# A fixed order from attention into the experts: second expert's weights in the keys' place, four early tiles of it before the last rows

## The chip, the cores and the metric

The kernel runs on one core of a Trainium2 chip. The metric is the device time in microseconds of one execution, as the median of several runs. Beside the plain runs there is one execution under the hardware profiler, from which all durations of instructions come.

## The reference

One transformer block over 4096 tokens (2 sequences of 2048, width 256) in float32. First attention with 16 heads of 64 in a causal window of 128 keys, then a mixture of 8 experts with two chosen for each token, both behind a layer norm whose scale and shift come from a small modulation vector:

```python
h = _layernorm(x) * (1 + ca) + sa
x = x + ga * attention(h, Wqkv, Wout)          # window of 128, softmax
h = _layernorm(x) * (1 + cb) + sb
probs = softmax(h @ gate_w.T + gate_b); topk_prob, topk_idx = top_k(probs, 2)
for c in range(2):                             # first and second choice
    pos  = how many earlier tokens chose the same expert as choice c
    keep = pos < 640                           # capacity
    hmid = relu(rows @ W1[e] + b1[e])          # 256 -> 1024
    y   += (hmid @ W2[e] + b2[e]) * prob * keep
x = x + gb * y
```

A token's place in its expert's buffer depends on all tokens before it. So the router of the last tokens is known only when attention and its output projection for them are done.

## The kernel before

**Numbers.** Each float32 operand is split into a high and a low part in the fp32r format (`split`: ScalarE casts the high part, a second engine subtracts it for the low part), and each product is made of three matmuls (`passes`, L203). The weights are loaded in pieces of 512 KB into two staging buffers (tag `raw`) and split from there.

**Attention.** The 4096 tokens are 16 groups `g` of 256. Work runs in iterations `w` = 0 to 63, each for two of the eight head pairs of a group; an iteration of the steady state takes 10.6 to 11 us. `iteration(w)` writes four ages of work beside one another: projections for w+1, scores of w, exponentials and scaling of w-1, transposes and values of w-2, output projection of w-3. Three more iterations, 64 to 66, empty this pipeline. The projections' weights `wq` lie in the tag `big` of pool `bigw`, the keys `kr` in the attention pool. The last projections of queries and keys are in w=62, those of values in w=63.

**Router.** `close(g)` is a generator of about ten steps for one group: residual (L620, L621), norm, transposes `tp_f`, logits `pl`, first and second choice, running counts `pref` and the matmuls `cnt`, slots, and at last four indirect DMAs on POOL (L785) that scatter the rows into `xbuf` in DRAM, where each expert has its region of 1280 rows. `place` gives each step an iteration and a point in it (letters A, B, H, C), `go` runs what is placed there. The last two groups are treated apart so that some rows can be read before they are known: `shift` moves late rows of expert 0 behind its first four tiles of 128 rows (`EARLY`), whose area the late scatters leave alone.

**Experts.** Work is cut into `items`: some tiles of one expert. Expert 0 has items 0 to 4 of two tiles each, experts 1 to 6 begin with an item of six tiles, and expert 7 with one of four. An item turns its rows (`turn_slots`, matmuls `tp_x`, split into `xT`), multiplies eight slices `f` of the first layer (`ph`; ReLU on ScalarE L904 and VectorE L905; low part L906, which for item 0 is POOL's), and two slices later the second layer (`y`). `results` adds the bias, `scale_of` makes each row's factor `gw` and destination `tok`, and `give` multiplies and adds the rows into the output by indirect DMAs on POOL (L967, L968). Items 0, 1, 2 and the head of each further expert always run; others run if `fill`, the count of rows, says so (`further`, L1178, behind a branch). With these inputs expert 0 and expert 1 have six tiles at most.

**Order.** Iterations 0 to 63 are written in a manual schedule: PE, ACT, DVE and POOL do their work in the order of the program. From iteration 64 on the framework's scheduler sets each engine's order, except where the program raises a priority (`go`) or keeps an order. Expert 0's weights go to the tag `big`, expert 1's to a tag `odd` of the expert pool `mp`, which opens when attention's pools close. The halves of expert 1's first matrix are split by ScalarE and POOL in items 1 and 2. SP issues nearly all loads and the output write of `close`, one behind the other; each waits there for its buffer and for what it reads.

Of the kernel before, what the change touches and what calls it, by code (L numbers as in the profile page):

```python
# [28 lines left out]
def adaln_block_kernel(  # L29
# [38 lines left out]


    EARLY = 4 * P  # L70
    WIDE = 6
# [32 lines left out]
    tokid = const.tile([P, NT], I32, name="tokid")  # L104
    shift = const.tile([P, 1], FP, name="shift")
    fill = const.tile([P, E], I32, name="fill")
# [25 lines left out]

    def load_split(hi, lo, src, shape, name, scale=None, pool=stage, eng=nc.vector, keep=False):
        raw = pool.tile(shape, FP, tag="raw", name=f"raw_{name}", bufs=2)
        nc.sync.dma_start(out=raw, in_=src)
        split(hi, lo, raw, scale, eng, keep)

    def load_expert(e, pool, tag):

        w = pool.tile([P, 2, ND * FF + NF * D], FR, tag=tag, name=f"we_{e}", bufs=1)  # L140
        wa = w[:, :, 0 : ND * FF].rearrange("p a (k f) -> p a k f", k=ND)
        wb = w[:, :, ND * FF :].rearrange("p a (k d) -> p a k d", k=NF)

        def pieces():
            for i in range(2):
                s = slice(i * FF // 2, (i + 1) * FF // 2)
                load_split(
                    wa[:, 0, :, s], wa[:, 1, :, s], w1[e, :, s].rearrange("(k p) f -> p k f", p=P),
                    [P, ND, FF // 2], f"w1_{e}_{i}", keep=e > 0, eng=nc.gpsimd if e == 1 else nc.vector,
                )  # L150
                yield
            for i in range(2):
                s = slice(i * NF // 2, (i + 1) * NF // 2)
                load_split(
                    wb[:, 0, s, :], wb[:, 1, s, :],
                    w2[e, i * FF // 2 : (i + 1) * FF // 2, :].rearrange("(k p) d -> p k d", p=P),
                    [P, NF // 2, D], f"w2_{e}_{i}", keep=e > 0,
                )
                yield

        return wa, wb, pieces()

# [7 lines left out]
    within = aw.tile([P, P], I32, name="within")  # L170
    kr = aw.tile([P, 2, NP, 2 * SBT, P], FR, name="kr")
    cols = aw.tile([P, 2, ND, B], FP, name="cols")
# [433 lines left out]
    def close(g):  # L606
# [60 lines left out]
        def tile2(name, n=SBT):  # L667
            return small.tile([P, n], FP, tag=name, name=f"{name}_{g}", bufs=2)
# [54 lines left out]

        if g == NG - 2:

            total = totals(j0, n)
            nc.vector.tensor_scalar(shift, total[:, 0:1], -1.0, float(EARLY), ALU.mult, ALU.add)
            nc.vector.tensor_scalar(shift, shift, 0.0, None, ALU.max)
        nc.tensor.matmul(out=cnt[:, 0:n], lhsT=tri, rhs=ohf, start=True, stop=False)
# [41 lines left out]
        if late:  # L771
            rows_of = NSLOT - EARLY
            sel = tile2("sel", SBT * KC)
            nc.vector.tensor_scalar(
                sel, pk, float(E * P), shift[:, 0:1], ALU.is_equal, ALU.mult
            )
            nc.vector.tensor_tensor(pos_, pos_, sel, ALU.add)

# [19 lines left out]
        if g == NG - 1:  # L798

            total = totals(NT, n)  # L800
            nc.vector.tensor_tensor(total[:, 0:1], total[:, 0:1], shift, ALU.add)
            nc.vector.tensor_copy(fill, total)
# [4 lines left out]


    items = []
    for e in range(E):  # L810
        head = 2 if e == 0 else 4 if e == E - 1 else WIDE
        ends = [0, *range(head, NB + 1, 2)]
        items += [(e, range(lo, hi)) for lo, hi in zip(ends, ends[1:])]
# [7 lines left out]
    def load_b2(e):  # L821
        pool = mp if e else const
        b2s[e] = pool.tile([P, D], FP, tag="b2", name=f"b2_{e}")
        nc.sync.dma_start(out=b2s[e], in_=b2[e : e + 1, :].to_broadcast([P, D]))
# [19 lines left out]
    def turn_slots(q, n0):  # L844

        tiles = items[q][1]
        if n0 == 0:
            w = len(tiles)
            if q and (w > 2 or items[q - 1][0] == E - 1 and items[q - 1][1].start == 0):
                w = WIDE  # L850
            xTs[q] = [
                (mp if q else early).tile([P, ND, w * P], FR, tag=f"xT{i}{w}", name=f"xT{i}_{q}")
                for i in range(2)
            ]
        m = min(2, len(tiles) - n0)
        if m <= 0:
            return
        tp = bank(f"tp_x{q}_{n0}")
        tpv = tp.rearrange("p (d s) -> p d s", d=ND)
        for n in range(m):  # L860
            for d in range(ND):
                turned = nc.tensor.transpose(
                    tpv[:, d, n * P : (n + 1) * P], xts[q][:, n0 + n, d * P : (d + 1) * P], ident
                )
                if q > 5:
                    tc.keep_in_program_order(turned)
        s = slice(n0 * P, (n0 + m) * P)
        split(xTs[q][0][:, :, s], xTs[q][1][:, :, s], tpv[:, :, 0 : m * P])

    def first_layer(q, f):  # L870
        e, tiles = items[q]
        wa = experts[e][0]
        xh, xl = xTs[q]
# [13 lines left out]
        for i in range(nw):  # L887
# [17 lines left out]
            nc.vector.tensor_scalar(r[:, s], phv, bias, 0.0, ALU.add, ALU.max)  # L905
        (nc.vector if q else nc.gpsimd).tensor_tensor(hl, r[:, 0:W], hh, ALU.subtract)  # L906
        hms[q, f] = (hh, hl)

    def second_layer(q, f, only=None):
        e, tiles = items[q]  # L910
        wb = experts[e][1]
        hh, hl = hms[q, f]
# [50 lines left out]
    def give():  # L963
# [27 lines left out]
    NW = NU // 2  # L991
    VALUES = [(0, 0), (1, 0), (0, 1), (1, 1)]

    NORM = ["0B", "1A", "1H", "2A", "2B"]
    CLOSE = ["0H", "1A", "1B", "2H", "3H", "4A", "4B", "5H", "6A", "6C"]
    LATE = {
        NG - 3: ["0H", "1A", "1B", "2H", "3H", "4A", "4B", "4H", "4C", "4C"],
        NG - 2: ["0H", "1A", "1B", "2H", "2H", "2C", "2C", "3H", "3C", "3C"],
        NG - 1: ["0H"],
# [7 lines left out]
    for g in range(NG):  # L1007
# [3 lines left out]
        place(last, g * (NP // 2) + 6, LATE.get(g, CLOSE))  # L1011

    def go(w, at):
        for work in places.pop((w, at), ()):
            if w < NW:
                next(work, None)
            else:
                with tc.high_priority():
                    next(work, None)

    def first_item():
        turn_slots(0, 0)
        yield
        for f in range(NF + LAG):
            if f < NF:
                first_layer(0, f)
            if f >= LAG:
                second_layer(0, f - LAG)
            yield
        results(0, 0, 2)  # L1030

# [3 lines left out]
    def iteration(w):  # L1035
# [37 lines left out]
        if w < NW:  # L1073
            project_v(g, *VALUES[p2])
        if done[1]:
# [19 lines left out]

    STEPS = {NW: 3, NW + 1: 4, NW + 2: 4}
    start = first_item()
    experts = {}
    part(*project_qk(0, 0, 1))
    everything = {mybir.EngineType.PE, mybir.EngineType.Activation, mybir.EngineType.DVE, mybir.EngineType.Pool}  # L1100
    with tc.manual_schedule(engines=everything):
        for w in range(NW):
            iteration(w)
            if w == NW - 2:
                load_b2(0)
                load_slots(0)
    experts[0] = load_expert(0, bigw, "big")
    for _ in experts[0][2]:
        pass
    for w in range(NW, NW + 3):  # L1110
        iteration(w)
        if w == NW + 2:
            load_slots(1)
        for _ in range(STEPS[w]):
            next(start, None)
    for _ in start:
        with tc.high_priority():
            next(last, None)
    for _ in last:
        pass  # L1120
    give()
# [5 lines left out]
    ring.update(pool=pm_, bufs=2)  # L1127
    experts[1] = load_expert(1, mp, "odd")
    load_b2(1)
    turn_slots(1, 0)  # L1130

    def item(q, steps):
# [26 lines left out]
    def start_expert(e):  # L1159
        if e < E and e not in experts:  # L1160
            experts[e] = load_expert(e, *((bigw, "big") if e % 2 == 0 else (mp, "odd")))
            load_b2(e)

    def piece(e):
        start_expert(e)
        if e < E:
            next(experts[e][2], None)

# [6 lines left out]
    def further(q):  # L1175

        e, tiles = items[q]
        with tc.If(filled[e] > tiles.start * P):  # L1178
# [5 lines left out]
    filled = []  # L1184
    item(
        1,
        {
            **{f: [do(piece, 1)] for f in range(2)},
            2: [do(load_slots, 2, 2)],
            4: [do(load_slots, 5)],  # L1190
            7: [do(turn_slots, 2, 0)],
        },
    )
    item(
        2,
        {
            0: [do(piece, 1)],
            1: [do(piece, 1)],
            7: [do(turn_slots, 3, 0)],
            4: [do(turn_slots, 5, 0)],  # L1200
            5: [do(turn_slots, 5, 2), fills],
            6: [do(turn_slots, 5, 4)],
        },
    )
    further(3)
    heads = [q for q in range(5, NI) if items[q][1].start == 0]
    for q, q2 in zip(heads, heads[1:] + [NI]):
# [38 lines left out]
```

## Time and profile before

| | |
|---|---|
| median of 3 runs | 1177.53 us (1176.76 to 1178.51) |
| the profiled execution's own time | 1175.13 us |
| its span, first to last instruction | 1173.1 us |
| mean granted clock of TensorE | 0.967 |
| busy: PE, DVE, ACT, POOL | 93%, 74%, 58%, 51% |
| scores of w=62 begin | 722.78 us |
| last group's residual ends | 769.97 us |
| first multiplication of item 1 | 790.26 us |
| first multiplication of item 2 | 808.66 us |
| first multiplication of expert 1 (six tiles) | 829.23 us |
| first multiplication of expert 2 | 868.41 us |

The profiled execution and its span differ by 2 us that lie outside the instructions. Times of events count from the first instruction. An engine's share of busy time is a mean over stages that have different limits; "busy" of TensorE contains time at a lowered clock, in which the same matmul takes longer.

### The profile page before, as it was taken

The numbers are of one execution on the slowest core, as the hardware profiler recorded it, in microseconds if no ns is written. First come the engines' busy times: TensorE is split into PE (matmuls) and PEld (weight loads), VectorE is DVE, ScalarE is ACT, GpSimd is POOL, SyncE is SP. The second block draws the span as 40 slices with busy tenths as digits, with TensorE's granted clock in tenths as the row PEclk, the third lists the DMA queues.
The fourth block names the chain that finished last, engine by engine and source line by source line (L and its number), as shares of the span: only waits on it lengthen the run. The fifth ranks groups of instructions, "written<-read, shape, count | busy, mean of one in ns | idle before, by whom it ended". The sixth has DMA issues, their size and how long they took to land. (4 is left out here: it accounts for less than half of the span.)

```text
span 1173.1 us, 25151 instructions
## 1 busy us (share of the span) xinstructions
PE 1090.8 (93%) x9244; PEld 1003.0 (86%) x9244; DVE 864.5 (74%) x2130; ACT 678.8 (58%) x2097; POOL 601.7 (51%) x777
## 2 busy tenths in 40 slices
PE   6899999999999989999999999868899999999995
PEld 4688888888988879889889888658899999999995
DVE  6556778778778777787787787758578777877774
ACT  4467677776776657777777676514344344444441
POOL 4235474674674555665665665554234606343524
PEclk9799999999999989999999999778899999999998
DMA  6991010010010010000000001315234524352413
GB/s 230 226 200 36 7 33 19 24 36 19 21 39 19 21 37 25 29 23 23 26 23 23 27 15 34 91 39 163 73 113 103 86 85 90 79 92 64 82 47 36
DMA packets 59571, 72.09 MB, mean 61 GB/s; under 512 B 4807, under 2 KB 51152, under 8 KB 59436
## 3 DMA queue, kind: packets, MB, share of 16 engines
q1 hardware_dynamic: 36988, 44.27, 12.3%
q0 software_dynamic: 11712, 14.79, 7.4%
q10 hardware_dynamic: 10736, 11.27, 4.2%
q8 instruction: 80, 1.31, 0.5%
q14 instruction: 55, 0.45, 0.1%
HBM read 40.11 MB, written 32.27 MB: 62 GB/s over the span
## 5 line engine op out<-in xcount | busy, mean ns | idle before, releaser
L523 ACT ACTIVATE pm<-pm,mx 128x128 f32<-128x128 f32 x512 | 204.1, 402 | 34.1 <-DVE mx L509 31.5
L904 ACT ACTIVATE hm<-ph,b1T 128x384 fp32r<-128x384 f32 (+2 forms) x184 | 99.3, 540 | 213.0 <-PE ph L203 178.3
L203 PE MATMUL pq<-hh,wq 128*128 128x256 f32 x1024 | 217.6, 296 | 4.1 <-ACT hh L239 3.7
L203 PE MATMUL y<-we,hm 128*128 128x256 f32 x1440 | 202.3, 286 | 10.1 <-DVE hm L906 6.8
L557 POOL TENSOR_SCALAR_AFFINE_SELECT pT<-pT 128x512 f32<-128x512 f32 (+1 forms) x128 | 80.5, 629 | 254.5 <-ACT pT L556 254.4
L203 PE MATMUL ph<-xT,we 128*128 128x384 f32 (+2 forms) x1104 | 200.2, 323 | 8.0 <-PEq L1178 4.2
L203 PEld LDWEIGHTS y<-we,hm 128*128 128x128 f32 x1440 | 187.3, 191 | 14.5 <-DVE hm L906 9.7
L203 PEld LDWEIGHTS ph<-xT,we 128*128 128x128 f32 x1104 | 172.2, 194 | 11.1 <-issue 4.5
L203 PEld LDWEIGHTS pq<-hh,wq 128*128 128x128 f32 x1024 | 170.2, 193 | 6.7 <-ACT hh L239 4.1
L905 DVE TENSOR_SCALAR r<-ph,b1T 128x384 f32<-128x384 f32 (+2 forms) x184 | 101.5, 562 | 72.0 <-ACT hm L904 57.9
L580 PE MATMUL av<-pT,v 128*64 128x128 f32 (+1 forms) x1472 | 130.3, 323 | 23.1 <-DVE pm L500 15.0
L533 POOL TENSOR_TENSOR pm<-pm,rd 128x512 f32<-128x512 f32 x128 | 133.5, 1043 | 27.8 <-DVE rd L531 27.8
L203 PE MATMUL pq<-hl,wq 128*128 128x256 f32 x512 | 145.8, 285 | 0.0
L499 ACT COPY pm<-sc 128x256 f32<-128x256 f32 (+1 forms) x256 | 80.8, 362 | 107.3 <-PE sc L475 70.4
L967 POOL TENSOR_TENSOR ys<-ys,gw 128x256 f32<-128x256 f32 x56 | 48.3, 968 | 182.3 <-DVE ys L957 177.7
L580 PEld LDWEIGHTS av<-pT,v 128*64 128x64 f32 x1472 | 92.2, 140 | 54.3 <-POOL h L636 17.8
L500 DVE COPY_PREDICATED pm<-within,sc 128x256 f32<-128x256 int32 (+1 forms) x256 | 95.8, 420 | 43.3 <-ACT pm L499 43.2
L968 POOL DMA_INDIRECT out_dram<-ys,tok x60 | 99.2, 1654 | 28.8 <-issue 12.2
L475 PE MATMUL sc<-kr,qh 64*128 64x256 f32 (+1 forms) x1024 | 104.3, 295 | 3.5 <-DVE ql L271 1.8
L523 ACT ACTIVATION_READ_ACCUMULATOR pm<-pm,mx 128x1 f32 x512 | 99.4, 194 | 0.0
L203 PEld LDWEIGHTS pq<-hl,wq 128*128 128x128 f32 x512 | 99.2, 194 | 0.0
L203 PE MATMUL po<-wo,ah 128*128 128x256 f32 x512 | 98.3, 285 | 0.0
(163 smaller groups left out, 2253.5 us busy)
## 6 DMA issues: line engine op xcount, KB each, us to landing
raw_w<-in_L_ffn_W_dram SPq DMA_DIRECT2D x32, 512.0 KB, 4.1
xbuf<-blank ACTq DMA_DIRECT2D x16, 685.0 KB, 8.7
xt<-xbuf SPq DMA_DIRECT2D x8, 822.0 KB, 5.0
x<-in_L_attn_x_dram SPq DMA_DIRECT2D x16, 256.0 KB, 2.8
out_dram<-x SPq DMA_DIRECT2D x16, 256.0 KB, 2.2
xt<-xbuf SPq DMA_DIRECT2D x7, 548.0 KB, 4.7
raw_wq<-in_L_attn_Wqkv_dram SPq DMA_DIRECT2D x6, 512.0 KB, 7.4
wm<-in_L_wmod_dram SPq DMA_DIRECT2D x1, 1024.0 KB
```

The source lines that it names most:

```text
L203: nc.tensor.matmul(out=out_, lhsT=a, rhs=b, start=start and n == 0 and i == 0, stop=stop and n == last and i == 2, **kw,)
L475: nc.tensor.matmul(out=sc[h][:, t, lo:], lhsT=q[r, t * P : (t + 1) * P], rhs=kr[r, (0, 1, 0)[i], hp, blk, :], start=(i == 0), stop=(i == 2),)
L499: nc.scalar.copy(pm[:, h, ts, :], blocks[:, own, :])
L500: nc.vector.copy_predicated(pm[:, h, ts, :], within.rearrange("p (a k) -> p a k", a=1).to_broadcast([P, n, P]), blocks[:, before, :],)
L523: nc.scalar.activation(pm[:, h, t, :], pm[:, h, t, :], AF.Exp, bias=mx[:, h, t : t + 1], accum_out=den[:, h, t : t + 1],)
L533: nc.gpsimd.tensor_tensor(pmv, pmv, rd.rearrange("p h (t a) -> p (h t) a", a=1).to_broadcast([P, 2 * SBT, P]), ALU.mult,)
L557: nc.gpsimd.affine_select(out=pT[:, :, t0:, 0, :], in_=own[:, :, t0:, :], pattern=[[0, 2], [0, n], [-1, P]], compare_op=ALU.is_gt, fill=0. ...
L580: nc.tensor.matmul(out=av[h * DH : (h + 1) * DH, q0 : q0 + hi - lo], lhsT=v[:, f0 + h * DH : f0 + (h + 1) * DH], rhs=pT[:, h, lo:hi], star ...
L904: nc.scalar.activation(hh[:, s], phv, AF.Relu, bias=bias)
L905: nc.vector.tensor_scalar(r[:, s], phv, bias, 0.0, ALU.add, ALU.max)
L967: (nc.vector if items[q][0] == E - 1 else nc.gpsimd).tensor_tensor(y, y, gw_, ALU.mult)
L968: add = nc.gpsimd.indirect_dma_start(out=of, out_offset=bass.IndirectOffsetOnAxis(ap=tok[:, 0:1], axis=0), in_=y, in_offset=None, bounds_c ...
```

## The change

It writes one order by hand from the last iterations of attention through items 0, 1 and 5 (the first items of experts 0 and 1); the scheduler takes over at item 2. In detail:

- `kr` moves to `bigw`, tag `odd`, and the weights of each odd expert take this place. So expert 1's weights can be split as soon as the last scores are made, inside iterations 64 to 66.
- Loading and splitting become two steps, `get` and `use`, in a class `Expert`; for experts 0 and 1 two pieces are asked for ahead. Expert 0's pieces are used at 63A, 63B, 63C and 64A, expert 1's at 65A, 65C, 66A and 66C. All low parts are VectorE's.
- The last value projection moves from w=63 to w=62 (`LAST_VALUES`), so that `wq` is free one iteration earlier.
- The steps of `close` for groups 13 and 14 move: the scatter of 13 from 62C to 61C, that of 14 to 65C. A new point M lies between the two output projections.
- Item 0 is placed slice by slice from 62A on; its low parts move from POOL to VectorE.
- The last router, after its norm, runs one step for each slice of item 1. It closes the early rows of expert 1 as well as of expert 0: `shift` has two columns.
- Expert 1 begins with four tiles (item 5), which run before item 2 (tiles 4 and 5 of expert 0). Its tiles 4 and 5 are item 6, after the branch of expert 0. Expert 2's four pieces and the turns of its first six tiles, which stood in the six-tile item of expert 1, are now in item 6.

```diff
-    shift = const.tile([P, 1], FP, name="shift")
+    shift = const.tile([P, 2], FP, name="shift")
...
-    kr = aw.tile([P, 2, NP, 2 * SBT, P], FR, name="kr")
+    kr = bigw.tile([P, 2, NP, 2 * SBT, P], FR, tag="odd", name="kr")
...
+        def steps(self):
+            ahead = 2 if self.e < 2 else 0
+            for i in range(ahead):
+                self.get(i)
+            if ahead:
                 yield
+            for i in range(4):
+                if not ahead:
+                    self.get(i)
+                self.use(i)
+                if ahead and i + ahead < 4:
+                    self.get(i + ahead)
                 yield
...
-        if g == NG - 2:
+        if late:
+            e = g - (NG - 2)
             total = totals(j0, n)
...
-            nc.vector.tensor_scalar(
-                sel, pk, float(E * P), shift[:, 0:1], ALU.is_equal, ALU.mult
-            )
-            nc.vector.tensor_tensor(pos_, pos_, sel, ALU.add)
+            for e in range(g - (NG - 2) + 1):
+                sel = tile2("sel", SBT * KC)
+                nc.vector.tensor_scalar(
+                    sel, pk, float((E - e) * P), shift[:, e : e + 1], ALU.is_equal, ALU.mult
+                )
+                nc.vector.tensor_tensor(pos_, pos_, sel, ALU.add)
...
-        head = 2 if e == 0 else 4 if e == E - 1 else WIDE
+        head = 2 if e == 0 else 4 if e in (1, E - 1) else WIDE
...
-        (nc.vector if q else nc.gpsimd).tensor_tensor(hl, r[:, 0:W], hh, ALU.subtract)
+        nc.vector.tensor_tensor(hl, r[:, 0:W], hh, ALU.subtract)
...
-    VALUES = [(0, 0), (1, 0), (0, 1), (1, 1)]
+    VALUES = [[(0, 0)], [(1, 0)], [(0, 1)], [(1, 1)]]
+    LAST_VALUES = [[(0, 0)], [(1, 0)], [(0, 1), (1, 1)], []]
...
     LATE = {
-        NG - 3: ["0H", "1A", "1B", "2H", "3H", "4A", "4B", "4H", "4C", "4C"],
-        NG - 2: ["0H", "1A", "1B", "2H", "2H", "2C", "2C", "3H", "3C", "3C"],
+        NG - 3: ["0H", "1A", "1B", "2B", "2H", "3A", "3B", "3H", "3C", "3C"],
+        NG - 2: ["0H", "1A", "1B", "2A", "2H", "2C", "3A", "3B", "3M", "3C"],
         NG - 1: ["0H"],
     }
...
+    place(experts[0].pieces, NW - 4, ["0A", "3A", "3B", "3C", "4A"])
+    place(experts[1].pieces, NW, ["0B", "1A", "1C", "2A", "2C"])
+    place(first, NW - 2, ["0A", *"2M 2H 2C 3A 3B 3M 3C 4A 4B".split()])
...
-    with tc.manual_schedule(engines=everything):
-        for w in range(NW):
-            iteration(w)
...
+    order = tc.manual_schedule(engines=everything)
+    order.__enter__()
+    for w in range(NW + 3):
+        iteration(w)
+    next(last)
+    next(first)
+    next(last)
+    next(first)
+    next(first, None)
     give()
     attn.close()
...
+    second = layers(1)
+    for f in range(NF + LAG + 1):
+        next(last, None)
+        next(second, None)
+        if f in (6, 8):
+            turn_slots(5, f - 6)
+    load_slots(2, 2)
+    load_slots(6, 2)
+    third = layers(5)
+    for f in range(NF + LAG + 1):
+        next(third, None)
+        if f == 0:
+            give()
+        if f == 6:
+            turn_slots(2, 0)
+    order.__exit__(None, None, None)
...
+    item(2, {0: [give], 3: [fills], 4: [do(turn_slots, 6, 0)], 6: [do(turn_slots, 3, 0)]})
     further(3)
+    more = {f: [do(piece, 2)] for f in (0, 2, 4, 6)}
+    more[1] = [do(load_slots, 9)]
+    more[7] = [do(turn_slots, 7, 0)]
+    for i in range(3):
+        more.setdefault(4 + i, []).append(do(turn_slots, 9, 2 * i))
+    item(6, more)
+    further(7)
```

## The prediction

> **What bounds the kernel now.** I read the whole execution first, then the stretch that the change rebuilds. The 40 slices show where TensorE is not busy: digits of 8 and 9 almost everywhere, and a dip in slices 26 to 28 (733 to 821 us) where its granted clock dips too.
>
> ```profile
> PE   6899999999999989999999999868899999999995
> ...
> DVE  6556778778778777787787787758578777877774
> ...
> PEclk9799999999999989999999999778899999999998
> ```
>
> Then the busy time by stage around that dip: engines' busy us with instruction counts, and after them the granted clock, DMA share and GB/s. I set the limits at events: last attention iterations, item 0, last router, item 1 (792 to 809), item 2 (809 to 825), the branch, expert 1 (829.3 to 868.4).
>
> ```profile
> core 0: us, PE busy (x) PEld busy (x) DVE busy (x) ACT busy (x) POOL busy (x), PEclk, DMA share, GB/s
> 722.00:730.00 8.00, 6.19 (x69) 5.21 (x69) 7.52 (x29) 3.41 (x13) 3.02 (x3) 1.00 0.13 44
> 730.00:742.00 12.00, 7.74 (x67) 6.11 (x66) 8.24 (x17) 7.80 (x23) 10.41 (x15) 0.84 0.53 156
> 742.00:756.00 14.00, 12.71 (x68) 10.71 (x67) 10.00 (x38) 7.39 (x25) 5.27 (x6) 0.53 0.26 80
> ...
> 779.00:792.00 13.00, 5.59 (x26) 4.85 (x26) 9.12 (x44) 1.71 (x4) 6.95 (x8) 0.63 0.20 23
> 792.00:809.00 17.00, 14.71 (x97) 14.50 (x97) 13.35 (x20) 7.41 (x14) 7.33 (x8) 0.78 0.65 205
> 809.00:825.00 16.00, 14.33 (x111) 13.05 (x109) 13.84 (x25) 7.72 (x15) 4.79 (x4) 1.00 0.38 82
> ...
> sum 146.40, PE 119.33 PEld 110.49 DVE 102.96 ACT 58.67 POOL 59.60; mean PE 11.93 PEld 11.05 DVE 10.30 ACT 5.87 POOL 5.96
> ```
>
> In these 146.4 us TensorE is busy 119.3, partly at about half clock; weighting each stage by its clock leaves some 103 us of work at full speed. VectorE is busy 103.0. So both have about 43 us of slack: the stretch is bound by neither, but by the order in which they wait for each other. The waits of TensorE there (us, times, longest) name the places:
>
> ```profile
> PE cnt L729 <- DVE oh L694: 5.6, 1, 5.6
> PE av L580 <- POOL pT L561: 4.4, 2, 4.3
> PE ph L203 <- PEq L1178: 4.2, 1, 4.2
> ...
> PE y L203 <- DVE hm L906: 2.3, 1, 2.3
> ```
>
> The first is the last router: nothing but tiny VectorE operations from 779 to 790, TensorE 43% busy. The second is attention's last selections on POOL behind a scatter and its neighbours. The third is the register load of the row counts with the first branch. The fourth is a collision, to be seen in the order of time (start, duration):
>
> ```profile
> 794.80 5.13 DVE L906 TENSOR_TENSOR hm<-r,hm 128x256 fp32r<-128x256 f32 x1
> ```
>
> In the same moment POOL runs its two weight subtractions of expert 1 (794.92, 4.71 us for both). The same VectorE operation takes 0.42 us elsewhere.
>
> [...] Here a 4.26 us wait at 735 to 739 is followed by ten microseconds at 0.50[...]; the router's operations last 0.17 and start 0.21 apart when dependent. No routing step is cheap by being small.
>
> **The change, part by part**, as a new timetable for 722.8 to 868.4, where expert 2's first matmul starts; what follows is the same code. Prices are start-to-start spacings in this trace: six 256-wide matmuls 0.71 (924.79, 925.49, 926.20); six 512-wide 1.38 (720.19 to 721.57); VectorE relu plus low part of 256 columns 1.05 (800.03, 801.08, 802.13); weight split 1.14 (737.60 to 738.74); xT or ys 0.60; gw 0.40; dependent router operation 0.21.
>
> 1. *Entry.* The last value projection moves from w=63 to w=62: +1.38. Group 13's router moves one iteration earlier (61 instead of 62), which takes 0.5 of cnt matmuls and about 4 us of VectorE work (723.1 to 727.1) out of w=62. But w=61 then asks 11.3 us of VectorE (16 selection operations 3.6, wt/kept/slot steps 2.7, packing 3.4, low parts 1.2, rest 0.4) in an iteration of 10.6 to 11: I charge 1.5. Scores of w=62 start at 722.8 + 1.38 - 0.5 + 1.5 = 725.2.
> 2. *w=63.* ACT's four exps (2.0), copies (1.2) and first weight cast end near 732.4; VectorE's first split frees the raw buffer near 733.2; the third raw piece lands 4.1 later (the page's median for raw_w) at 737.3, is cast by 738.3; behind it on ACT wait the four score copies (1.2), then packing and two maxima (3.1): last maximum at 742.6, against 746.3 before. Releasing wq early hides the first two pieces, but not this one.
> 3. *w=64 to 66.* VectorE's written order holds 22.4 us: low parts of item 0, now here and no longer on POOL (8 x 0.95 = 7.6; with waits 1.05), group 14's router 7.7 (pick, count, slots, shift), expert 1's first three splits 3.4 and expert 0's last 1.1 (expert 1's first half leaves POOL: two times 2.40 there become 1.14 each here), xT 0.6, six attention residues 2.0. Waits: about 1.5 for expert 0's last cast, 1.3 for the last exps, 0.7 for ph, 1.5 for counts: 5. Group 15's residual ends at 770, against 769.97 before. Nothing gained so far: the 3.7 us go into VectorE's added work.
> 4. *To item 1.* In order on VectorE: last split 1.14, statistics 1.2, POOL's root about 1.1, normalization 1.06, two row operations 1.22, ys 0.6, two gw 0.8, xT 0.6, handovers: 9 us, 779. TensorE's next instruction, the router's transposes, waits for most of it, and the multiplications of item 1 stand behind. Before, item 1 began at 790.26.
> 5. *Item 1 over the router.* VectorE: 8 x 1.05 + the router, 8.0 (780.10 to 788.85 less two gw) + 1.0 for the second shift (a totals matmul, four operations and a select with its add) + gw 0.8, xT_5 1.2, ys 0.6 = 20 against TensorE's 14.2 (48 matmuls of each kind at 0.118 make 11.4, router and turns 2.8). VectorE sets the end: 799. Before, item 2 began at 808.66. The collision of 5.13 is gone, as no POOL subtraction is left.
> 6. *Item 5, four tiles of expert 1.* TensorE 8 x 1.38 + 16 x 0.71 + turns 0.8 = 23.2, one more for the cold clock: 823. It covers slots, POOL's four scatters (4 x 1.28) and the two row loads behind the counts on SP's queue (5.0 each): done near 813, wanted at 815 to 820.
> 7. *Item 2 and branch.* 13.0 (as 903.81 to 916.80) and 4.2 unchanged: 840.
> 8. *Item 6.* All of expert 2's splits, formerly inside a six-tile item of 39 us, and the turns of its first six tiles now fall into a two-tile item: VectorE 8 x 1.05 + 4 x 1.14 + 4 x 0.60 + 0.8 + 0.6 = 16.8; item 2 before needed 16 us for 13.84 busy with such a mixture, so 18.5 to 19. With the branch 1.1: expert 2 at 860.5.
>
> The matmuls are the same number of tiles: expert 0 ran six and expert 1 six before, and run 2+2+2 and 4+2. Gain: 868.4 - 860.5 = 7.9. The profiled execution took 1175.13 for a span of 1173.1; it becomes 1167.2, and the median of the runs stands 2.4 above it: **1169.6**.
>
> Queues passed: on SP the last group's output write and item 5's row load now stand behind expert 1's pieces and one or two of expert 2's; free near 772, landed at 778, wanted at 793. On POOL item 0's scaling and two scatter-adds (782.15 to 789.5 before) precede the last scatter, but that is not ready before 794. If this cover fails, item 5 or 2 starts late by the excess.
>
> **Costs that the trace doesn't show.** Handovers of a rigid order: from 0 (my waits suffice) to 1 us for each of 16 hidden slices of items 0 and 1; I take 0, for the steps count waits already. Row load and raw pieces of expert 2 squeezed into item 6: 842 KB and two times 512 KB at the 205 GB/s of 792 to 809 take 9.1 us, within 18.5; from 0 to 5 us if issued late behind the branch; I take 0.
>
> **Rivals.**
> - *More gained.* If TensorE runs ahead so that the 5 us of waits in step 3 and half of the 9 us in step 4 vanish, and item 6 needs only its 16.8: some 12 us more, 1157. For it: VectorE's busy sum stays near 104 us of 146. Against: one written order per engine, where each wait blocks all that is behind it.
> - *Slower.* Head-of-line blocking in the written order: TensorE stands at pl, cnt and tp_f while finished multiplications queue behind, and cools to half clock. Place: w=64 to item 1. Price: up to 1 us per slice, 16 us; it decides from 0.5 us per slice on, when the gain is eaten. At 0.9: 6 us slower, 1184. For it: before, 742 to 756 ran at 0.53 with 91% busy. Against: a blocked slice has ready work on the other side.
> - *A wash.* Expert 2's loads late in item 6: 5 us, and three more for the crowded VectorE: 1177.
>
> **How the numbers follow.** Likeliest (1162 to 1174) 0.54, more gained 0.20, wash 0.08 (two thirds of it within 0.2%), slower 0.18. A measurement of this kernel tells about 0.2%, 2.4 us, from no change. Faster 0.74, same 0.06, slower 0.20 (the wash's far side included). Range 1154 to 1183.
>
> **What would show it.** Right: item 1's first multiplication near 779 instead of 790; no wait of several us at cnt; VectorE 90% busy in item 1; item 6 longer than item 2; expert 2 near 860. Wrong: item 1 starts after 785 (step 3 or 4), item 5 waits for rows (cover of SP and POOL), item 6 beyond 22 us (step 8), or a difference before 715 us, where I expect none.

## The result, and the profile after

| | before | after |
|---|---|---|
| median of 20 runs each, one chip | 1179.38 us (1175.08 to 1183.47) | 1184.43 us (1179.09 to 1190.15) |
| ratio, 95% interval | | 1.0043 (1.0027 to 1.0059) |
| span of the profiled execution | 1173.1 us | 1185.7 us |
| first multiplication of item 1 | 790.26 us | 793.42 us |
| first multiplication of expert 2 | 868.41 us | 877.54 us |

The changed kernel is slower by 0.43%, 5 us. The forecast was 1169.6 us: a gain of 7.9 on the 1177.53 that was known then, and 10 us below the 1179.38 of this chip.

The 40 slices of the profile after, TensorE, VectorE and TensorE's granted clock:

```profile
PE   6799999999999989999999999678889999999995
...
DVE  6556768778778767787787777767567877777774
...
PEclk9799999999999989999999999779989999999998
```

The dip is still there. Counting slices from 1, TensorE is below 9 in slices 26 to 30; before it was so in 26 to 29 (the prediction gave 26 to 28). In digits nothing was filled up. The waits of TensorE in the rebuilt stretch, 722 to 881 us (what waited, for whom, total us, times, longest; PEq is TensorE's sequencer, `issue` a wait for nothing that the profile shows):

```profile
PE tp_f L676 <- DVE h L663: 5.3, 1, 5.3
PE cnt L761 <- DVE both L746: 4.6, 2, 2.8
PE ph L232 <- PEq L1230: 4.4, 1, 4.4
PE y L232 <- DVE hm L938: 3.3, 4, 1.4
...
PE ph L232 <- issue: 2.7, 2, 2.5
```

The 5.6 us wait at `cnt` (for `oh`) of before has shrunk to 1.0, and the 5.13 us collision in item 1 is gone. In their place stand two new ones: the transposes `tp_f` of the last rows (5.3), and the counts behind the totals (`both`, 4.6 in two). Here is the first of these two, in TensorE's order of time:

```profile
764.90 0.29 PE L741 MATMUL cnt<-pref,ones 128*128 128x16 f32 x2
767.97 0.64 PE L761 MATMUL cnt<-oh,tri 128*128 128x32 f32 x2 [2.77 <-DVE both L746]
768.41 0.61 PE L762 MATMUL cnt<-pref,ones 128*128 128x32 f32 x2
```

and in VectorE's:

```profile
765.75 1.22 DVE L127 TENSOR_TENSOR we<-raw_w,we 128x1024 fp32r<-128x1024 f32 x1
766.88 0.48 DVE L937 TENSOR_SCALAR r<-ph,b1T 128x256 f32<-128x256 f32 x1
767.40 0.42 DVE L938 TENSOR_TENSOR hm<-r,hm 128x256 fp32r<-128x256 f32 x1
767.74 0.17 DVE L746 TENSOR_SCALAR both<-cnt 128x16 f32<-128x16 f32 x1
```

The totals' matmul ends at 765.2. VectorE could read its result (`both`, 0.17 us), but in the written order a weight split, a ReLU and a low part of item 0 stand ahead of it. The next count matmul goes into the same PSUM tile and waits until `both` is read; the multiplications of item 0 and the output projections, whose operands are there, queue behind it. What that costs beyond the wait is in the clock (windows: busy us with counts for five engines, then granted clock, DMA share, GB/s):

```profile
765.00:768.00 3.00, 0.23 (x4) 0.13 (x2) 2.83 (x10) 0.74 (x2) 2.45 (x3) 0.91 0.00 0
768.00:775.00 7.00, 7.00 (x35) 7.00 (x36) 3.25 (x17) 1.08 (x3) 0.32 (x1) 0.55 0.26 75
790.00:800.00 10.00, 7.52 (x32) 6.86 (x33) 5.17 (x14) 2.63 (x7) 5.09 (x5) 0.50 0.32 76
```

After the wait TensorE is busy for all of seven microseconds, at 0.55 of its clock (a clock near one half is called cold below): 7 x 0.45, an estimated 3.1 us lost on top of 2.8. This is the dearest of three profiles of this kernel: in the two others the wait is 2.5 and half clock lasts only 3.4 us behind it (766.1 to 769.5 in the second profile), so 2.5 + 1.7. The third row is the same behind the wait at `tp_f`: the beginning of item 1 at 0.50.

### The profile page after: what moved, and what is told of

Same layout as the page of the kernel before. It is cut to its first block, busy times and chain, and to the rows that moved or that the text cites. A ratio compares the mean times of both kernels' runs of the same rounds, so it can differ in the third digit from the quotient of the medians.

```text
span 1185.7 us, 25167 instructions
## 1 busy us (share of the span) xinstructions
PE 1092.0 (92%) x9246; PEld 1004.6 (85%) x9246; DVE 873.7 (74%) x2154; ACT 679.0 (57%) x2097; POOL 591.6 (50%) x767
## 5 line engine op out<-in xcount | busy, mean ns | idle before, releaser
L936 ACT ACTIVATE hm<-ph,b1T 128x256 fp32r<-128x256 f32 (+2 forms) x184 | 99.0, 539 | 228.5 <-PE ph L232 196.9
L232 PE MATMUL ph<-xT,we 128*128 128x256 f32 (+2 forms) x1104 | 205.7, 328 | 13.4 <-PEq L1230 4.4
L232 PEld LDWEIGHTS ph<-xT,we 128*128 128x128 f32 x1104 | 174.6, 199 | 19.0 <-issue 7.8
L937 DVE TENSOR_SCALAR r<-ph,b1T 128x256 f32<-128x256 f32 (+2 forms) x184 | 101.9, 563 | 76.3 <-ACT hm L936 68.8
L609 PE MATMUL av<-pT,v 128*64 128x128 f32 (+1 forms) x1472 | 128.4, 319 | 22.9 <-DVE pm L529 15.9
L504 PE MATMUL sc<-kr,qh 64*128 64x256 f32 (+1 forms) x1024 | 104.3, 294 | 6.0 <-DVE ql L300 2.9
L552 ACT ACTIVATION_READ_ACCUMULATOR pm<-pm,mx 128x1 f32 x512 | 98.8, 193 | 0.0
L938 DVE TENSOR_TENSOR hm<-r,hm 128x256 fp32r<-128x256 f32 (+2 forms) x144 | 94.2, 654 | 5.3
```

The lines of the kernel that those rows point to most:

```text
L232: nc.tensor.matmul(out=out_, lhsT=a, rhs=b, start=start and n == 0 and i == 0, stop=stop and n == last and i == 2, **kw,)
L504: nc.tensor.matmul(out=sc[h][:, t, lo:], lhsT=q[r, t * P : (t + 1) * P], rhs=kr[r, (0, 1, 0)[i], hp, blk, :], start=(i == 0), stop=(i == 2),)
L552: nc.scalar.activation(pm[:, h, t, :], pm[:, h, t, :], AF.Exp, bias=mx[:, h, t : t + 1], accum_out=den[:, h, t : t + 1],)
L609: nc.tensor.matmul(out=av[h * DH : (h + 1) * DH, q0 : q0 + hi - lo], lhsT=v[:, f0 + h * DH : f0 + (h + 1) * DH], rhs=pT[:, h, lo:hi], star ...
L936: nc.scalar.activation(hh[:, s], phv, AF.Relu, bias=bias)
L938: nc.vector.tensor_tensor(hl, r[:, 0:W], hh, ALU.subtract)
```

## How the runs are compared

Executions of one and the same kernel differ by up to 10 us (before: 1174 to 1184), and the two profiles above differ by 12.6 us of span against 5 us of the medians. So positions in the rebuilt stretch are counted from the same event in each profile, the copy of the 61st value projection, which stands just ahead of it:

```profile
700.16 0.59 ACT L289 COPY v<-pv 128x512 f32<-128x512 f32 x1 [0.79 <-PE pv L203]
```

```profile
709.54 0.59 ACT L318 COPY v<-pv 128x512 f32<-128x512 f32 x1 [0.75 <-PE pv L232]
```

The first is of before, the second of after: the difference of 9.4 us lies ahead of all that the change rebuilds. The first question was therefore whether it belongs to the change. The marks of all profiles, in us from that copy (several numbers are several profiles of the same kernel):

| kernel | last residual ends | item 1's first ReLU | item 5's first ReLU | expert 2's first ReLU |
|---|---|---|---|---|
| before | 69.8, 69.3 | 92.3, 90.9 | | 169.6, 166.2 |
| kr_place | 69.7 | 91.3 | | 168.1 |
| before_counts | 68.5 | 90.6 | | 168.8 |
| after | 75.5, 74.2, 74.4 | 86.1, 84.7, 85.0 | 108.9, 106.5, 109.3 | 172.6, 170.0, 173.0 |
| low_pool | 76.3 | 86.8 | 108.6 | 171.2 |
| counts_first | 71.1 | 81.6 | 102.7 | 166.2 |
| ahead_only | 73.3 | 80.7 | 104.3 | 167.2 |
| ahead_gw | 74.3 | 79.4 | 103.7 | 165.8 |
| ahead_counts | 71.0, 69.9 | 76.7, 75.1 | 99.6, 98.6 | 162.5, 161.1 |
| all_three | 71.6 | 77.3 | 100.0 | 166.3 |
| raw_early | 70.0 | 75.7 | 98.6 | 161.2 |

From expert 2's first ReLU to the end the kernels take 302.0 to 304.6 us, before 302.9 in the mean (kr_place with it) and after 303.9.

The forecast counts to another event, the first multiplication of expert 2. It comes at 168.3 and 164.3 in before, 166.7 in kr_place, and 168.0, 165.5 and 168.6 in after: 166.4 and 167.4 in the mean. From there to the first ReLU it takes 1.4 to 2.0 us in before and kr_place, and 4.4 to 4.6 in after. So of the 5 us of loss about 1 lies ahead of expert 2's first multiplication, about 3 right behind it, and about 1 in the rest. What stands behind those 3 is taken up in the last experiment.

## The experiments

Three theories stood at the start. T1: the loss is in the rebuilt stretch, by waits in the written order. T2: attention itself became slower, because the keys and all behind them lie elsewhere in SBUF. T3: the difference in attention is chance, between executions.

**Is attention slower?** Both kernels were run again, unchanged:

> The kernel before, unchanged, as a measure of how far one execution's profile differs from another of the same instructions. T1 (the loss lies in the rebuilt stretch, in-order waits) and T3 (the attention of one profiled execution simply differs from that of another) expect a ratio of 1.000 and, between the two profiles of this kernel, a drift of the 61st iteration's value copy of several us (it started at 700.16 us in the first profile). T2 (tile placement slows attention by a fixed amount) expects the same ratio, but the value copy of the 61st iteration again within 2 us of 700.

> The changed kernel, unchanged. All theories: ratio 1.004 (1184 against 1179). T2: the 61st iteration's value copy again near 709.5 us, as in the first profile, that is about 9 us behind the kernel before. T3: it moves towards 700 to 705 in at least one more profile, with the total moving by as much.

Measured: before again 0.9997 (0.9981 to 1.0013), after again 1.0037 (1.0020 to 1.0053). The 61st value copies came at 705.25 in before, against 700.16 in its first profile, and at 707.26 in after against 709.54. A third profile of after had it at 703.33. The two ranges of this mark overlap, 700.16 to 705.25 and 703.33 to 709.54.

The place of the keys alone, in the kernel before:

```diff
-    kr = aw.tile([P, 2, NP, 2 * SBT, P], FR, name="kr")
+    kr = bigw.tile([P, 2, NP, 2 * SBT, P], FR, tag="odd", name="kr")
...
-    experts[1] = load_expert(1, mp, "odd")
+    experts[1] = load_expert(1, bigw, "odd")
...
-            experts[e] = load_expert(e, *((bigw, "big") if e % 2 == 0 else (mp, "odd")))
+            experts[e] = load_expert(e, bigw, "big" if e % 2 == 0 else "odd")
```

> The kernel before with only the place of the keys changed: they lie in the buffer that the odd experts' weights take later, as in the changed kernel; the order of work stays. T2: slower by 5 to 10 us, 1184 to 1189, with the loss ahead of 715 us. T1 and T3: no difference in attention; the odd experts' weights have the same size and come at the same time, so 1177 to 1181.

Measured: 0.9988 (0.9977 to 1.0000), value copy at 703.39. Not slower.

Attention alone, both kernels cut off after iteration 59 (for before the same lines in its manual schedule):

```diff
-    for w in range(NW + 3):
+    for w in range(60):
         iteration(w)
...
+    attn.close()
```

> The kernel before, cut off after the first 60 attention iterations; the last six iterations, the experts and all their output are left out. It is the base for the next kernel. From the three profiles of the order of before (61st value copy at 700.2, 705.3 and 703.4 us) some 690 us, with several us between executions.

> The changed kernel, cut off at the same place: the same instructions with the same waits in the same order on every engine as the cut kernel before; only the addresses in SBUF differ. T2 (the changed kernel's attention is slower through where its tiles lie): 3 to 6 us above the cut kernel before. T3 (single profiles differ by chance, the loss lies behind attention): within 1 us of it.

Measured: 712.65 us (710.58 to 713.00, 5 runs) and 711.62 us (710.14 to 713.78, 5 runs). The forecast of some 690 us was 22 too low, and the cut kernels are not quite the attention of the full ones: their 60th value copy comes at 700.6 in the cut kernel before, against 688.3 and 693.1 in the full one; why is not known. The full kernels say the same of T2, though: with the keys in the new place the 61st copy comes between 699.0 (ahead_counts, second time) and 709.5 us, twelve profiles with a mean of 703.9; with the old place it comes at 700.2, 705.3 and 702.8. T2 has fallen: attention costs the same in both within a microsecond or so, and the 9.4 us of the two first profiles are chance. In the marks the stretch from the 61st value copy to expert 2 takes 3.9 us more (means 171.9 against 168.0 with kr_place), which leaves one of the 5 us for the rest, within the spread there.

**Is it VectorE's sum?** Item 0's low parts back on POOL:

```diff
-        nc.vector.tensor_tensor(hl, r[:, 0:W], hh, ALU.subtract)
+        (nc.vector if q else nc.gpsimd).tensor_tensor(hl, r[:, 0:W], hh, ALU.subtract)
```

> The changed kernel with one part undone: the eight low-part subtractions of item 0 go back to POOL (0.95 us each on VectorE in the last attention iterations). If VectorE's work there is what sets the end (step 3 of my sum, 7.6 us of added work), the last residual ends some 5 us earlier and the time is 3 to 6 us lower, 1179 to 1181. If the waits of the written order set it, the time stays within 2 us of 1184[...].

Measured: 1.0048 (1.0034 to 1.0062), beside 1.0037 (1.0020 to 1.0053) of after on the same chip: not faster. The last residual ends at 76.3, not earlier. The edit took less off VectorE than the expectation says: the low part alone lasts 0.42 us, and the 0.95 contains the ReLU, which stayed; so eight operations made 3.4 us, not 7.6. Two waits of TensorE show what ate them:

```profile
764.34 0.64 PE L761 MATMUL cnt<-oh,tri 128*128 128x32 f32 x2 [2.61 <-DVE both L746]
779.92 0.73 PE L232 MATMUL y<-we,hm 128*128 128x256 f32 x4 [1.74 <-POOL hm L938]
```

The wait at the counts is still there, as the split and the ReLU still stand ahead of `both`. And on POOL a low part, 0.74 us there, now stands behind four scatters and comes late. So this run alone does not tell whether VectorE's sum sets the pace, as it lengthened another queue; all_three below is the cleaner test.

**Does the wait at the counts cost?** The count matmuls ahead of the totals, by moving one block:

```diff
-        if late:
-            e = g - (NG - 2)
-            total = totals(j0, n)
-            ...
         nc.tensor.matmul(out=cnt[:, 0:n], lhsT=tri, rhs=ohf, start=True, stop=False)
         nc.tensor.matmul(
             ...
         )
+        if late:
+            e = g - (NG - 2)
+            total = totals(j0, n)
+            ...
         sm = tile2("sm")
```

> The changed kernel with one edit: the count matmuls are issued before the totals' matmul instead of behind it, so that TensorE does not wait in the two late routers until VectorE has read the totals (4.8 us in 2 waits). T1: TensorE's next layers start 2.5 us earlier each time; 2 to 4 us faster, 1180 to 1182. Rival (VectorE's queue sets the pace in w = 64 to 66 and in item 1, TensorE only waits for it): within 1 us of the changed kernel.

Measured: 0.9993 (0.9983 to 1.0002); against 1.0037 to 1.0043 of after that is 5 to 6 us, more than T1 expected. The place in TensorE's order of time, and the seven microseconds behind it:

```profile
757.10 0.31 PE L753 MATMUL cnt<-oh,tri 128*128 128x32 f32 x2
757.58 0.41 PE L754 MATMUL cnt<-pref,ones 128*128 128x32 f32 x2 [0.17 <-DVE pref L730]
757.82 0.37 PE L741 MATMUL cnt<-pref,ones 128*128 128x16 f32 x2
758.04 0.95 PE L232 MATMUL ph<-xT,we 128*128 128x256 f32 x6
```

```profile
757.00:764.00 7.00, 6.83 (x59) 6.58 (x59) 6.38 (x24) 3.30 (x7) 2.64 (x3) 1.00 0.24 75
```

The wait of 2.77 is 0.17, the clock stays at 1.00, and TensorE issues 59 matmuls where after issued 35. VectorE does 6.38 us of work instead of 3.25: in after it stood in this stretch waiting for ScalarE's ReLUs (1.51 and 1.82 us), and these for TensorE (4.82 and 3.37). The last residual ends 3 to 4.4 us earlier, item 5 starts 4 to 7 us earlier.

The same edit in the kernel before, whose totals stand in one router only:

> The kernel before with the same edit of the counts (its totals stand in group 14's router only; the profile shows VectorE and TensorE waiting for each other there for 1.3 and 0.8 us). T1 (the wait costs because the written order holds ready multiplications behind it): here the planner put other work around it, so less than 1 us, 0.999 to 1.000. Rival (the wait itself costs, whatever the order): 2 us faster, 0.998.

Measured: 1.0005 (0.9993 to 1.0017). There the order in iterations 64 to 66 is the scheduler's, and the edit brings nothing. That fits T1, but is no proof of it, since that wait was also shorter (0.8 us of TensorE).

**Does the wait at `tp_f` cost?** Item 1 ahead of the last router, first with a second buffer for item 0's `gw`, then without it:

```diff
-        gw_ = pool.tile([P, D], FP, tag="gw", name=f"gw_{q}_{n}", bufs=6 if q else 1)
+        gw_ = pool.tile([P, D], FP, tag="gw", name=f"gw_{q}_{n}", bufs=6 if q else 2)
...
     next(first)
-    next(last)
     next(first)
...
     turn_slots(1, 0)
+    next(last)
     second = layers(1)
     for f in range(NF + LAG + 1):
-        next(last, None)
         next(second, None)
+        next(last, None)
```

> The changed kernel with item 1 ahead of the last router: its input is turned before the last rows are normalized, in each pair of slices the layers stand before the router's step, and item 0's scaling factors get a second buffer. T1 (in-order waits eat the gain): the wait of 5.3 us at tp_f goes, and with it the cold clock of item 1 (22.8 us became 20 in my sum), so 4 to 7 us faster than the changed kernel, 1177 to 1180. Rival (the chain of the last router sets the end, item 1 only fills it): the router's end and item 5's rows come as late or later, no gain, 1183 to 1186.

> The changed kernel with item 1 ahead of the last router, as in ahead_gw, but without the second buffer for item 0's scaling factors, so that ACT still waits some 9 us for POOL there and the cast of item 1's input behind it comes late. If the order alone brings the gain: 0.9997 of the kernel before again. If the buffer brings part of it: item 1's first multiplication some 3 to 5 us later than in ahead_gw, and 1.001 to 1.003.

Measured: 0.9997 (0.9989 to 1.0006) with the buffer, 1.0008 (0.9995 to 1.0021) without. So the order brings most of it, and the buffer's part, some 0.1%, is not told apart by these intervals. In the marks item 1 starts 5 to 7 us earlier than in after with both, 4 to 5 with the order alone. T1 was right on the time, but not on the clock: TensorE now waits at item 1's own input instead (2.8 us for VectorE in ahead_gw, 4.8 for ScalarE in ahead_only), and in ahead_gw the granted clock is still 0.50 from 782.5 to 792.7.

**Do the two add?** With after beside them on the same chip:

> The changed kernel, unchanged, on the same chip as the three that follow. All theories: ratio 1.004 to the kernel before, as in its two earlier measurements.

> Both edits of the last two experiments in one kernel: item 1 ahead of the last router, and count matmuls ahead of the totals. Alone they brought 0.9997 and 0.9993 of the kernel before, where the changed kernel has 1.004. If the two waits are separate places (T1), the gains add: 0.995 of the kernel before (some 5 us faster). If both only let TensorE reach the same later limit (the rows of item 5, VectorE in item 1), they do not add: 0.999 to 1.000.

> As ahead_counts, and the second half of expert 1's weight splits (two subtractions of 1.2 us on VectorE, two casts of 1.05 us on ACT) moved out of the last attention iterations into item 5, whose second layers are the first to read them. If VectorE's length in w = 64 to 66 still sets the end, 2 us less than ahead_counts. If waits set it, no difference (within 1 us).

Measured: after 1.0039 (1.0026 to 1.0053), ahead_counts 0.9963 (0.9953 to 0.9973), all_three 0.9981 (0.9971 to 0.9992). The two edits (ahead_counts has the second buffer of ahead_gw, too) bring 0.0076 together, 9 us, most of their sum (0.0046 for the counts, 0.0042 for item 1 ahead). all_three, which moves expert 1's second half into item 5, is slower than ahead_counts by 2.2 us in the means. Its last residual ends at 71.6, against 71.0 and 69.9: with two splits fewer on VectorE the end does not come earlier, so VectorE's sum does not set it in this order. TensorE in item 5 of all_three, in the order of time:

```profile
807.89 0.28 PE L232 MATMUL y<-we,hm 128*128 128x256 f32 x1
810.02 2.02 PE L232 MATMUL y<-we,hm 128*128 128x256 f32 x11 [1.85 <-DVE we L127]
811.84 2.70 PE L232 MATMUL ph<-xT,we 128*128 128x512 f32 x6
```

The second layer now waits 1.85 us for the split, and six 512-wide matmuls take 2.53 from start to next start, instead of 1.38, at a granted clock of 0.50 from 812 to 814: again a wait with a cold clock after it, in a place that had none. Neither branch of the expectation, 2 us gained or no difference, came true.

**Why does item 6 take longer than summed?** In ahead_counts, with ahead_counts itself once more beside it:

```diff
-            ahead = 2 if self.e < 2 else 0
+            ahead = 2 if self.e < 3 else 0
...
-    item(2, {0: [give], 3: [fills], ...
+    item(2, {0: [give], 2: [do(piece, 2)], 3: [fills], ...
```

> As ahead_counts, and the first two raw pieces of expert 2's weights are loaded in item 2, ahead of the branch, instead of behind it in item 6 (step 8 of my sum took 0 for late loads; ACT waited 2.1 and 0.4 us for them in item 6 of ahead_counts, and the last second layers waited 3.3 us for VectorE). If the late loads make item 6 long: from the branch to expert 2 2 to 3 us less, 2 to 3 us faster than ahead_counts. If VectorE's sum there (16.8 us in my sum) sets it: within 0.7 us of ahead_counts.

> The same as ahead_counts, beside raw_early on one chip: 0.996 of the kernel before again, as there.

Measured: 0.9956 (0.9943 to 0.9969) and 0.9955 (0.9939 to 0.9970), medians 1168.10 and 1168.11 us beside 1173.67 of before. Earlier loads of the first two pieces bring nothing; ScalarE then waits 2.0 us for a later one, so the experiment does not show what item 6 would be with no late load at all. What is missing in the sum stands behind item 6, in TensorE's order of time in after:

```profile
877.54 0.61 PE L232 MATMUL ph<-xT,we 128*128 128x384 f32 x2 [0.84 <-DVEq L1230]
880.62 1.76 PE L232 MATMUL ph<-xT,we 128*128 128x384 f32 x5 [2.47 <-issue]
```

After two matmuls of expert 2 TensorE stands for 2.5 us, and nothing that it waits for shows in this view. All eleven profiles with the new order have this stall, of 1.4 to 2.5 us; in before's order it is 0 to 0.4. The record of DMA packets in the traces shows what goes with it. In each of the eleven a packet of 16 KB on the queue that the profile calls "instruction" (q8) starts 2.2 to 2.4 us before the matmul that ends the stall, whatever the stall's length: 0.2 to 0.7 us behind expert 2's first multiplication. In before's order the same packet starts 0.8 to 1.8 us ahead of expert 2's first multiplication, and where it was the latest, 0.8 (before's second profile), there is a stall too, of 0.42, which ends 2.2 us after the packet's start. That TensorE waits after the branch for what this packet brings is my estimate, from these near-constant 2.2 to 2.4 us and the queue's name. No experiment moved the packet, and why it starts later in the new order stays open.

The version that beats both kernels is ahead_counts: 0.9963 and 0.9955 of before in two measurements, some 5 us faster than before and 9 faster than after.

## Why the prediction was wrong, step by step

Counted from the 61st value copy (the forecast's times less 700.16), forecast and first profile of after (the terms of step 7 add up to 17.2 and those of step 8 to 19.6 to 20.1; the forecast's times were rounded):

| step | forecast ends at | forecast takes | measured ends at | measured takes |
|---|---|---|---|---|
| 2, last maximum | 42.4 | | 42.9 | |
| 3, w=64 to 66 | 69.8 | 27.4 | 75.5 | 32.6 |
| 4, to item 1 | 78.8 | 9 | 83.9 | 8.4 |
| 5, item 1 over the router | 98.8 | 20 | 106.6 | 22.8 |
| 6, item 5 | 122.8 | 24 | 129.5 | 22.9 |
| 7, item 2 and branch | 139.8 | 17.0 | 148.2 | 18.7 |
| 8, item 6, to expert 2's first multiplication | 160.3 | 20.5 | 168.0 | 19.8 |
| behind it: two matmuls and the stall | | | 171.1 | 3.1 |

- **Steps 1 and 2 held** (scores of w=62 at 24.8 against 25.0, last maximum at 42.9 against 42.4), and steps 4 and 6 to about a microsecond. The collision is gone, as said.
- **Step 3 failed**, by 5.2 us. Its term "1.5 for counts" counted the wait on VectorE. It left out TensorE, which stands behind `both` for 2.8 us with finished operands queued, and the cold clock after it. With that wait taken away the step takes 28.1 us (43.0 to 71.1 in counts_first), 0.7 from the sum.
- **Step 5 failed**, by 2.8 us. I took item 1 as bound by VectorE, at 20 us, 90% busy, with a cold clock charged to item 5 only. VectorE was busy for 15.84 of the 22.76 us, 70%, and TensorE's clock was 0.74 in the mean. Item 1 began at a clock of 0.50 after the 5.27 us at `tp_f`, which step 4 named as a wait and gave no price, and it has the second wait at the totals (1.8).
- **Step 7** is 1.5 over its terms. **Step 8** is 0.7 under, to the event that it names; behind that event stands the stall, which the forecast took as "the same code" and whose 3 us it had nowhere. The term "late loads, 0 to 5, I take 0" was not refuted.
- The base was a little long as well: before's first profile has 169.6 to expert 2's first ReLU where two others of that order have 166.2 and 168.1. About 1.6 us of the forecast gain came from this one execution.
- The rival "Slower" named what happened: TensorE at `cnt` and `tp_f`, finished work behind it, half clock, from w=64 to item 1. Its price at 0.9 us per slice was 1184; that this is also the measured figure is luck in part, as about 3 us of the loss are the stall at expert 2, which the rival does not contain. What I held against it, that a blocked slice has ready work on the other side, is the error: work on the other side of a blocked instruction stands behind it in the same queue (TensorE busy for 0.23 of the 3 us from 765 to 768). The term "handovers of a rigid order: I take 0" is where it should have been charged.
- With the wait at the counts gone and that at `tp_f` cut to 0.8 to 1.3 us (ahead_counts) the stretch to expert 2's first multiplication is 9.1 us shorter than in before (157.3 against 166.4 in the mean), where 7.9 were forecast; to the first ReLU, behind the stall, it is 6.2 shorter. So a reordering of this kind is worth about what was summed, and in after the two waits took it away, with the stall on top. But ahead_counts is a different order from the forecast one, and it still has a wait of 3.2 us at item 1's input.
- The clock was priced too mildly. The forecast charged one microsecond for it, in item 5. Here waits of 2.77 us (after) and 1.85 us (all_three) came with half clock of 6.8 and 3.4 us. A wait's length alone doesn't tell whether one comes: the wait for `hm` at item 1's start in before is 2.29 us in one profile, with 3.4 us at half clock (799.5 to 803.0), and 2.28 in another, followed by none (1.00 from 801 to 811). What decides was not shown, as no experiment varied it. The way back was priced too mildly as well: with the 4.26 us wait of before, to which the prediction gives ten microseconds at 0.50, the clock stays at 0.50 for 17.1 us (738.1 to 755.2), with TensorE busy for 14.5 of them.

## What to carry to other kernels

When an order is written by hand, go through each engine's queue and ask of every instruction that waits for another engine what ready work stands behind it; price it as the wait plus the cold clock that can follow, here 2.8 + 3.1 us in one profile and 2.5 + 1.7 in the other two. A tiny operation that another engine waits for (0.17 us for `both`) belongs ahead of the long ones in its own queue (not tried here), or the instruction that waits for it belongs behind work that is ready (counts_first, 5 to 6 us). And before a difference of two profiles is explained, look at whether it lies ahead of the first instruction that the change moves.

## What the runs showed of the hardware

- A wait of TensorE of 1.85 us (all_three) and one of 2.77 us (after) came with half clock, of 3.4 and 6.8 us (from 767.5 to 774.3 in after); one of 2.28 (before's second profile) and one of 2.35 (after's second) did not, and with one of 2.58 (after, until 745.58) the clock stayed at 1.00 until the next wait, at 746.7. In the first profiles of before and after the twelve stretches at half clock between 700 and 900 us last 3.4, 6.8, 13.7 or 17.1 us.
- Moving eight subtractions of 0.42 us off a busy VectorE to POOL, where one took 0.72 to 0.74, gave nothing (1.0048 against 1.0037 to 1.0043); one of them came late behind four scatters of POOL.
- Two executions of identical instructions can be 5 us apart by the 61st iteration (700.16 and 705.25, both of before).
- After the branch ahead of expert 2 TensorE stood 1.4 to 2.5 us after its second matmul, until 2.2 to 2.4 us after a 16 KB packet on the instruction queue had started (eleven profiles).
